# Graph attention, list building: adj added onto column fractions by the transfer itself, instead of a plain load, a conversion on ScalarE and a product on GpSimd

## The chip, the cores and the metric

The kernel runs on one core of one Trainium2 chip. The metric is the device time of one execution in microseconds (us). An execution can fall in a slower state; ratios and intervals use fast runs alone. The kernels before and after were compared first on one chip; the experiments ran later on two others, on which the kernel before takes 1408 to 1439 us, slow runs included, instead of 1363 to 1372. So an experiment's time is only compared with runs of the kernel before on the same chip, and stages are compared by the traces.

## The reference

```python
# x: 3327 x 1024 float32, adj: 3327 x 3327 int32, 0 or 1, symmetric, with ones on the diagonal, some 17 ones a row
h = jnp.maximum(_layernorm(x, axis=-1), 0.0)
f = h @ Wf + bf
g = h @ Wg + bg
e = jax.nn.relu(f @ g.T)
scores = jnp.where(adj > 0, e, NEG)
attention = jax.nn.softmax(scores, axis=1)
return x + attention @ (h @ W + bW)
```

## The kernel before

Because adj has few ones, the kernel does not form the 3327 x 3327 scores (a dense path for other inputs stands in the file and is not used here). **Stage 1** turns each 128-row tile of adj (26 tiles) into a list of up to 40 column numbers per row, normalises x into a table `hd` in DRAM, multiplies the two weight matrices, and ranks the rows by degree. **Stage 2** gathers the rows of `hd` by these lists, forms the dots, the softmax and the weighted sums, and projects. The change concerns stage 1. There, one tile of adj passes through four engines:

```python
kpool = pool1("key", 4)            # four buffers for r, 128 x 3327 float32
iotaj = c1.tile([P, N], FP, name="iotaj")       # 1, 2, ... 3327 in every row
held = p_c.tile([P, NBIN + KM], FP, name="held")  # p_c is PSUM
iotad, lst = held[:, :NBIN], held[:, NBIN:]

def degrees(t):
    n = rows(t)
    r = kpool.tile([P, N], FP, name="r")
    a = r.bitcast(I32)
    for b, m in pieces(t):
        nc.sync.dma_start(a[b : b + m], adj[t * P + b : t * P + b + m, :])
    # [cut: the last two tiles go in two parts]
    nc.scalar.activation(r[:n, b:e], a[:n, b:e], AF.Relu, accum_out=to)      # int32 to float32; the sum is the degree
    nc.gpsimd.tensor_mul(r[:n, b:e], r[:n, b:e], iotaj[:n, b:e])             # key: the column's number, or 0
    return r

def edges(t, r):
    n = rows(t)
    cand = cpool.tile([P, SEG * 8], FP, name="cand")
    for s in range(SEG):                        # 8 largest keys of each of 16 segments of 208 columns
        nc.vector.max(cand[:n, s * 8 : s * 8 + 8], r[:n, s * SW : min(N, (s + 1) * SW)])
    # [cut: count of keys above 0]
    for i in range(0, KM, 8):                   # the 40 largest of the 128 candidates, in order
        nc.vector.max(lst[:n, i : i + 8], cand[:n])
        if i + 8 < KM:
            nc.vector.match_replace(cand[:n], lst[:n, i : i + 8], cand[:n], 0.0)
    nc.vector.tensor_scalar(lst[:n], lst[:n], float(N), 1.0, op0=ALU.min, op1=ALU.max)
    nc.vector.tensor_scalar(pay[:n, t, :KM], lst[:n], -1.0, None, op0=ALU.add)
    # [cut: degree, and its one-hot row]

for t in range(NT):                             # NT = 26, LAG = 4
    r = degrees(t)
    normed(t)     # load of x, row statistics (odd tiles on DVE, even ones on ScalarE), store to hd
    edges(t, r)
    # [cut: ranks, stores of finished lists]
    if t < KD:                                  # KD = 8
        load_Wg(t)
    elif t < 2 * KD:
        make_A(t - KD)
    if t == 2 * KD:
        make_rows()   # bias rows: three tiny casts on DVE, some matmuls
# [cut: ranking of the rows; then stage 2, whose first act is a gather on GpSimd]
```

## Time and profile before

The time was 1364.33 us (median of 3 runs); the profiled run's span on the core was 1370.1 us. I call **seam** the moment at which GpSimd issues the first gather of stage 2: it ends stage 1. **DMA work** is the sum of the durations of all packets in the trace, divided by 16 engines.

| kernel before | us |
|---|---|
| last packet of adj ends | 237.2 |
| seam | 285.3 |
| length of stage 2 | 1084.8 |
| DMA work on adj | 117.3 |
| all DMA work until the last packet of adj | 207.5 |
| median packet of adj (13,308 bytes, one row) | 0.498 |

The stretches of the kernel before, which the prediction uses, read: start:end, length, then busy time of PE, weight loads, DVE, ACT and POOL with the number of instructions in brackets, the granted clock, the mean busy share of the DMA engines, and GB/s. The whole of stage 1 up to the last adj packet, in such a line:

```profile
15.00:237.00 222.00, 176.51 (x639) 109.60 (x639) 183.92 (x897) 155.03 (x234) 169.54 (x24) 0.97 0.87 329
```

DVE is busy for 184 of 222 us and the DMA engines for 0.87 of the time. How adj is loaded stands among the DMA issues (out<-in, issuing queue, operation, count, KB each, median us from issue to landing):

```profile
r<-in_adj_dram SPq DMA_DIRECT2D x25, 1663.5 KB, 9.0
```

### The profile page before, as it was taken

The page shows a single profiled execution, that of the slowest core. Times are in us where ns is not written, and L with a number is a line of the kernel's source. Part 1 is how long each engine was busy: PE and PEld are TensorE (multiplying, and loading weights), DVE is VectorE, ACT ScalarE, POOL GpSimd, SP SyncE. Part 2 cuts the span into 40 slices and gives each one's busy share as a digit, 9 for nine tenths or more (in the row PEclk, how much of TensorE's full clock was granted, in tenths as well). Part 3 has the DMA queues.
Part 4 walks back from the last instruction along what each step waited for, and adds up shares of the span by engine and source line. Part 5 has one row for each costly group of instructions (what it writes and reads, how often), then busy time and mean ns, then how long its engine had stood idle before and what let it go on. Part 6 is the DMA issues. An engine that isn't in the chain of part 4 may idle for free.

```text
span 1370.1 us, 14184 instructions
## 1 busy us (share of the span) xinstructions
PE 1154.2 (84%) x4355; PEld 676.0 (49%) x4355; DVE 1218.5 (89%) x2595; ACT 489.2 (36%) x774; POOL 875.0 (64%) x628
## 2 busy tenths in 40 slices
PE   4669899246467998999999999999979999999784
PEld 3545454124244564656555555555545555555331
DVE  4888888928869999999999899999999999999970
ACT  6677676501042542344433233333322222221110
POOL 7787778435456766677667767776656667666411
PEclk9999999568689999999999999999999999999897
DMA  9887898268558989898989988988877889888612
GB/s 367 356 336 281 320 351 276 68 257 327 172 166 302 348 294 320 299 334 292 309 290 311 303 269 312 302 294 296 272 240 250 255 281 306 272 271 285 198 32 63
DMA packets 97711, 372.52 MB, mean 272 GB/s; under 512 B 14269, under 2 KB 14685, under 8 KB 94298
## 3 DMA queue, kind: packets, MB, share of 16 engines
q0 software_dynamic: 79552, 286.85, 62.4%
q1 hardware_dynamic: 10860, 70.49, 13.6%
q10 hardware_dynamic: 7212, 14.18, 2.9%
q8 instruction: 36, 0.59, 0.2%
q14 instruction: 51, 0.41, 0.1%
HBM read 343.67 MB, written 27.80 MB: 271 GB/s over the span
## 4 chain that ended last, share of the span: by engine, by line
PE 43%; issue 14%; DVE 9%; DMA 4%; POOL 4%; ACT 2%; POOLq 0%; ACTq 0%; DVEq 0%
PE ps_q L666 18%; PE ps_o L758 17%; PE yT_ps L724 6%; DVE G L746 5%; DMA G<-hd,pi 4%; POOL G L637 3%; DVE junk L683 3%; PE ps_q L667 1%; PE ps_o L759 1%; ACT hT L650 1%; DMA pi<-pd,perm 1%; PE ps_t L649 1%; DVE sc L683 1%; POOL res L637 0%; ACT q L668 0%
## 5 line engine op out<-in xcount | busy, mean ns | idle before, releaser
L637 POOL DMA_INDIRECT G<-hd,pi x468 | 541.2, 1156 | 220.2 <-issue 93.5
L683 DVE CUSTOM_DVE_ANT_0 junk<-G,q 128x1024 bf16<-128x1024 f32 x468 | 599.4, 1281 | 35.3 <-ACT q L668 18.1
L666 PE MATMUL ps_q<-A_sb,hT 128*128 128x342 f32 x1248 | 399.2, 467 | 59.4 <-ACT q L668 41.8
L746 DVE SCALAR_TENSOR_TENSOR G<-G,sc 128x1024 f32<-128x1024 f32 x320 | 410.8, 1284 | 4.6 <-ACT G L744 4.1
L758 PE MATMUL ps_o<-W_sb,yT 128*128 128x512 f32 x832 | 374.8, 604 | 4.4 <-ACT yT L753 4.4
L666 PEld LDWEIGHTS ps_q<-A_sb,hT 128*128 128x128 f32 x1248 | 231.8, 194 | 177.6 <-ACT q L668 43.7
L758 PEld LDWEIGHTS ps_o<-W_sb,yT 128*128 128x128 f32 x832 | 156.5, 192 | 195.4 <-issue 182.3
L436 POOL TENSOR_TENSOR r<-r,iotaj 128x3327 f32<-128x3327 f32 (+4 forms) x28 | 188.6, 6743 | 66.6 <-ACT r L435 51.7
L724 PE MATMUL yT_ps<-ident,G 128*128 128x128 f32 x1184 | 146.2, 279 | 24.7 <-DVE sc L708 8.2
L446 DVE MAX8 cand<-r 128x8 f32<-128x208 f32 (+2 forms) x416 | 134.4, 361 | 35.2 <-POOL r L436 35.2
L724 PEld LDWEIGHTS yT_ps<-ident,G 128*128 128x128 f32 x1184 | 133.8, 143 | 41.8 <-issue 15.7
L760 ACT COPY res<-ps_o 128x512 f32<-128x512 f32 x52 | 30.4, 585 | 298.9 <-PE ps_o L759 298.9
L740 ACT ACTIVATE G<-G,sc 128x1024 f32<-128x1024 f32 x122 | 129.2, 1135 | 0.0
L668 ACT COPY q<-ps_q 128x342 f32<-128x342 f32 x78 | 33.5, 447 | 244.8 <-DVE sc L683 135.9
L519 PE MATMUL ps_A<-WgT,WfT 128*128 128x512 f32 x256 | 118.5, 623 | 2.7 <-ACT WfT L490 2.6
L637 POOL DMA_INDIRECT res<-in_x_dram,perm x26 | 46.2, 1776 | 67.4 <-ACT res L760 62.8
L519 PEld LDWEIGHTS ps_A<-WgT,WfT 128*128 128x128 f32 x256 | 50.6, 200 | 65.1 <-issue 61.2
L768 POOL DMA_INDIRECT out_dram<-res,perm x25 | 34.5, 1378 | 72.5 <-DMA res<-in_x_dram,perm 72.5
L435 ACT ACTIVATE r<-r 128x3327 f32<-128x3327 int32 (+4 forms) x28 | 77.5, 2768 | 0.1
L650 ACT COPY hT<-ps_t 128x512 f32<-128x512 f32 x52 | 28.9, 590 | 59.2 <-PE ps_t L649 32.0
L637 POOL DMA_INDIRECT hp<-hd,perm x26 | 26.8, 1032 | 35.0 <-DVE final L612 21.2
L649 PE MATMUL ps_t<-ident,hp 128*128 128x128 f32 x208 | 31.2, 292 | 15.7 <-issue 10.8
(137 smaller groups left out, 743.9 us busy)
## 6 DMA issues: line engine op xcount, KB each, us to landing
r<-in_adj_dram SPq DMA_DIRECT2D x25, 1663.5 KB, 9.0
xt<-in_x_dram SPq DMA_DIRECT2D x25, 512.0 KB, 9.8
hd<-xt ACTq DMA_DIRECT2D x25, 512.0 KB, 6.8
G<-hd,pi POOLq DMA_INDIRECT x468, 6.1
wr<-in_L_gnn_Wg_dram SPq DMA_DIRECT2D x8, 512.0 KB, 13.9
wr<-in_L_gnn_Wf_dram SPq DMA_DIRECT2D x8, 512.0 KB, 9.6
W_sb<-in_L_gnn_W_dram SPq DMA_DIRECT2D x1, 4096.0 KB, 16.3
r<-in_adj_dram SPq DMA_DIRECT2D x1, 1455.6 KB, 8.8
```

The lines of the kernel that those rows point to most:

```text
L435: nc.scalar.activation(r[:n, b:e], a[:n, b:e], AF.Relu, accum_out=to)
L436: nc.gpsimd.tensor_mul(r[:n, b:e], r[:n, b:e], iotaj[:n, b:e])
L446: nc.vector.max(cand[:n, s * 8 : s * 8 + 8], r[:n, s * SW : min(N, (s + 1) * SW)])
L519: nc.tensor.matmul(ps, WfT[:, k, :], WgT[:, k, o * CB : (o + 1) * CB], start=(k == 0), stop=(k == KD - 1))
L637: return nc.gpsimd.indirect_dma_start(out=to, out_offset=None, in_=table, in_offset=bass.IndirectOffsetOnAxis(ap=idx, axis=0), **kw,)
L649: nc.tensor.transpose(ps[:, k, :], of[:, (g + k) * P : (g + k + 1) * P], ident)
L666: nc.tensor.matmul(ps[:, :QB], hT[:, k, :], A_sb[:, k, o : o + QB], start=(k == 0), stop=False)
L683: nc.vector.tensor_tensor_reduce(junk, g, e["q"][:, :D], 1.0, e["q"][:, D : D + 1], op0=ALU.mult, op1=ALU.add, accum_out=e["sc"][:, k : k ...
L724: nc.tensor.matmul(e["yT"][:, c, :], g[:, c * P : (c + 1) * P], ident, is_transpose=True, start=(first and c % 4 == 0), stop=(last and c % ...
L740: nc.scalar.activation(g, g, AF.Copy, scale=p)
L746: nc.vector.scalar_tensor_tensor(y, g, p, y, op0=ALU.mult, op1=ALU.add)
L758: nc.tensor.matmul(ps, yT[:, k, :], W_sb[:, k, o * CB : (o + 1) * CB], start=(k == 0), stop=False)
```

## The change

The intent is to take work off the engines: the column fractions j/4096 are copied into the buffer, and the load of adj, cast from int32 to float32 on its way, is **added** onto them. What lands is the key: 1 + j/4096 for an edge, j/4096 otherwise. ScalarE then only counts signs of (key - 1), into another tile and beside DVE; GpSimd's product, and ScalarE's place between load and DVE, are gone.

```diff
+KEY = 4096.0
+        nc.vector.tensor_scalar(iotaj, iotaj, 1.0 / KEY, None, op0=ALU.mult)
-        def degrees(t):
+        def keys(t):
             n = rows(t)
             r = kpool.tile([P, N], FP, name="r")
-            a = r.bitcast(I32)
+            nc.gpsimd.tensor_copy(r[:n], iotaj[:n])
             for b, m in pieces(t):
-                nc.sync.dma_start(a[b : b + m], adj[t * P + b : t * P + b + m, :])
-            [cut: the last two tiles in two parts]
-                nc.scalar.activation(r[:n, b:e], a[:n, b:e], AF.Relu, accum_out=to)
-                nc.gpsimd.tensor_mul(r[:n, b:e], r[:n, b:e], iotaj[:n, b:e])
+                for c, e in ((0, SEG // 2 * SW), (SEG // 2 * SW, N)):
+                    nc.gpsimd.dma_start(
+                        r[b : b + m, c:e], adj[t * P + b : t * P + b + m, c:e], accum_op=ALU.add
+                    )
+            sign = lnj.tile([P, N], BF, name="sign")
+            nc.scalar.activation(sign[:n], r[:n], AF.Sign, bias=minus1[:n], accum_out=deg[:n, t : t + 1])
             return r
 [cut: the buffers minus1 and tops]
 [cut: count of keys above 1.0 instead of 0.0]
-            nc.vector.tensor_scalar(lst[:n], lst[:n], float(N), 1.0, op0=ALU.min, op1=ALU.max)
-            nc.vector.tensor_scalar(pay[:n, t, :KM], lst[:n], -1.0, None, op0=ALU.add)
+            nc.scalar.copy(tops[:n, t : t + 1], lst[:n, 0:1])
+            ids = cpool.tile([P, KM], FP, name="ids")
+            nc.vector.tensor_scalar(ids[:n], lst[:n], 1.0 + N / KEY, 1.0 + 1 / KEY, op0=ALU.min, op1=ALU.max)
+            nc.vector.tensor_scalar(pay[:n, t, :KM], ids[:n], KEY, -KEY - 1.0, op0=ALU.mult, op1=ALU.add)
 [cut: the degree is kept as 2 x degree - N, its uses are adapted]
-            r = degrees(t)
+            r = keys(t)
```

More of the change, by code (lines that the diff above doesn't have):

```diff
@@ L367, in edge_path @@
         nc.gpsimd.iota(iotaj, pattern=[[1, N]], base=1, channel_multiplier=0, allow_small_or_imprecise_dtypes=True)
+        nc.vector.tensor_scalar(iotaj, iotaj, 1.0 / KEY, None, op0=ALU.mult)
+        minus1 = c1.tile([P, 1], FP, name="minus1")
+        nc.gpsimd.memset(minus1, -1.0)
         iotap = c1.tile([P, P], FP, name="iotap")
@@ L372, in edge_path @@
         iotad, lst = held[:, :NBIN], held[:, NBIN:]
-        nc.vector.tensor_copy(iotad, iotap[:, :NBIN])
+        nc.vector.tensor_scalar(iotad, iotap[:, :NBIN], 2.0, -float(N), op0=ALU.mult, op1=ALU.add)
         part = c1.tile([P, 1], FP, name="part_no")
@@ L383, in edge_path @@
         deg = c1.tile([P, NT], FP, name="deg")
-        half = c1.tile([P, 1], FP, name="half")
+        tops = c1.tile([P, NT], FP, name="tops")
         cnt = c1.tile([P, NT], FP, name="cnt")
@@ L387, in edge_path @@
         oh = c1.tile([P, NT, NBIN], BF, name="oh")
-        nc.gpsimd.memset(deg, 1.0)
+        nc.gpsimd.memset(deg, 2.0 - N)
+        nc.gpsimd.memset(tops, 0.0)
         nc.gpsimd.memset(cnt, 1.0)
@@ L423, in normed @@
                 nc.scalar.dma_start(hd[t * P + a : t * P + a + m, :], xt[a : a + m])
-        def degrees(t):
+        def keys(t):
             n = rows(t)
             r = kpool.tile([P, N], FP, name="r")
-            a = r.bitcast(I32)
+            nc.gpsimd.tensor_copy(r[:n], iotaj[:n])
             for b, m in pieces(t):
-                nc.sync.dma_start(a[b : b + m], adj[t * P + b : t * P + b + m, :])
-            cuts = [0, SEG // 2 * SW, N] if t >= NT - 2 else [0, N]
-            for i, (b, e) in enumerate(zip(cuts, cuts[1:])):
-                to = deg[:n, t : t + 1] if not i else half[:n]
-                nc.scalar.activation(r[:n, b:e], a[:n, b:e], AF.Relu, accum_out=to)
-                nc.gpsimd.tensor_mul(r[:n, b:e], r[:n, b:e], iotaj[:n, b:e])
-                if i:
-                    nc.scalar.activation(deg[:n, t : t + 1], deg[:n, t : t + 1], AF.Identity, bias=half[:n])
+                for c, e in ((0, SEG // 2 * SW), (SEG // 2 * SW, N)):
[4 more added lines that the diff above has]
+            nc.scalar.activation(sign[:n], r[:n], AF.Sign, bias=minus1[:n], accum_out=deg[:n, t : t + 1])
             return r
@@ L448, in edges @@
             nc.vector.tensor_scalar(
-                pos[:n], cand[:n], 0.0, None, op0=ALU.is_gt, op1=ALU.add, accum_out=cnt[:n, t : t + 1]
+                pos[:n], cand[:n], 1.0, None, op0=ALU.is_gt, op1=ALU.add, accum_out=cnt[:n, t : t + 1]
             )
@@ L454, in edges @@
                     nc.vector.match_replace(cand[:n], lst[:n, i : i + 8], cand[:n], 0.0)
-            nc.vector.tensor_scalar(lst[:n], lst[:n], float(N), 1.0, op0=ALU.min, op1=ALU.max)
-            nc.vector.tensor_scalar(pay[:n, t, :KM], lst[:n], -1.0, None, op0=ALU.add)
+            nc.scalar.copy(tops[:n, t : t + 1], lst[:n, 0:1])
+            ids = cpool.tile([P, KM], FP, name="ids")
+            nc.vector.tensor_scalar(ids[:n], lst[:n], 1.0 + N / KEY, 1.0 + 1 / KEY, op0=ALU.min, op1=ALU.max)
+            nc.vector.tensor_scalar(pay[:n, t, :KM], ids[:n], KEY, -KEY - 1.0, op0=ALU.mult, op1=ALU.add)
             dg = cpool.tile([P, 1], FP, name="dg")
-            nc.vector.tensor_scalar(dg[:n], deg[:n, t : t + 1], float(NBIN - 1), None, op0=ALU.min)
+            nc.vector.tensor_scalar(dg[:n], deg[:n, t : t + 1], 2.0 * (NBIN - 1) - N, None, op0=ALU.min)
             nc.vector.tensor_copy(pay[:n, t, KM : KM + 1], dg[:n])
@@ L613, in edge_path @@
         ne = c1.tile([P, NT], FP, name="ne")
+        nc.vector.tensor_scalar(cnt, cnt, 2.0, -float(N), op0=ALU.mult, op1=ALU.add)
         nc.vector.tensor_tensor(ne, deg, cnt, op=ALU.not_equal)
+        nc.vector.tensor_scalar(tops, tops, 2.0, None, op0=ALU.is_ge)
+        nc.vector.tensor_max(ne, ne, tops)
         nc.vector.tensor_reduce(bads[:, NT : NT + 1], ne, AX.X, ALU.max)
-        nc.vector.tensor_scalar(ne, deg, 1.0, None, op0=ALU.is_lt)
+        nc.vector.tensor_scalar(ne, deg, 2.0 - N, None, op0=ALU.is_lt)
         nc.vector.tensor_reduce(bads[:, NT + 1 : NT + 2], ne, AX.X, ALU.max)
@@ L669, in prepare @@
         df = small.tile([P, 1], FP, name="df")
-        nc.vector.tensor_copy(df, pi[:, KM : KM + 1])
+        nc.vector.tensor_scalar(df, pi[:, KM : KM + 1], 0.5, N / 2, op0=ALU.mult, op1=ALU.add)
         nc.vector.tensor_scalar(bads[: rows(s), s : s + 1], df[: rows(s)], float(CAPS[s]), None, op0=ALU.is_gt)
```

## The prediction

> **What bounds the kernel now.** I first read the page's busy slices, then the busy time of the engines by stretches, then the waits of the first stage. The program has two stages. In the first, 26 tiles of adj (128 x 3327) become lists of keys while x is normalised and the weights are multiplied; in the second, rows are gathered by those lists. The change touches the first stage only (and one instruction per tile in the second). The seam is visible in the waits: GpSimd sits idle until `final`, then issues the first gather of the second stage, 285.3 us into the span (timeline of GpSimd).
>
> Stretches of the kernel before (start:end, length, then busy us of PE, weight loads, DVE, ACT, POOL; granted clock, DMA share, GB/s):
>
> ```profile
> 15.00:35.00 20.00, 11.69 (x55) 11.08 (x54) 13.34 (x56) 16.08 (x25) 18.10 (x3) 1.00 1.02 419
> 35.00:75.00 40.00, 22.06 (x105) 20.52 (x104) 33.19 (x169) 26.70 (x41) 28.73 (x5) 1.00 0.86 333
> ...
> 195.00:240.00 45.00, 42.33 (x138) 21.70 (x137) 39.29 (x195) 30.11 (x49) 35.48 (x5) 0.96 0.85 282
> 240.00:266.00 26.00, 6.44 (x61) 4.96 (x60) 25.05 (x110) 17.60 (x34) 14.76 (x4) 0.62 0.16 61
> 266.00:286.00 20.00, 2.76 (x35) 1.76 (x34) 16.24 (x52) 0.00 (x0) 0.67 (x1) 0.50 0.16 35
> ```
>
> The reader is to see that until 240 us both DVE (83 to 87%) and the DMA engines (0.85 to 1.02) are nearly full, and that from 240 to 286 us only DVE works: the last lists and the ranking. DVE's only large wait, and the loads' largest, are these:
>
> ```profile
> DVE cand L446 <- POOL r L436: 35.2, 15, 3.7
> ```
>
> ```profile
> SPq L430 <- DVE cand L446: 64.1, 9, 11.3
> ```
>
> So DVE waits 35.2 us in all for GpSimd's product, and the adj loads wait for DVE to free one of four buffers. The product itself, from the page:
>
> ```profile
> L436 POOL TENSOR_TENSOR r<-r,iotaj 128x3327 f32<-128x3327 f32 (+4 forms) x28 | 188.6, 6743 | 66.6 <-ACT r L435 51.7
> L446 DVE MAX8 cand<-r 128x8 f32<-128x208 f32 (+2 forms) x416 | 134.4, 361 | 35.2 <-POOL r L436 35.2
> ```
>
> The obvious prize is those 35 us. What counts against it is how little room the DMA engines have. Queues of the first 260 us (packets, MB, share of 16 engines):
>
> ```profile
> q1 hardware_dynamic: 9820, 66.30, 67.4%
> q10 hardware_dynamic: 6096, 13.00, 13.7%
> ```
>
> That is 0.674 x 260 = 175 us for adj, x and the weights, and 36 us for writing hd: 211 us of a stage whose loads end near 240.
>
> **What the Trainium skill says.** "DMA: Bandwidth & Descriptors", section SWDGE vs HWDGE vs iDMA: accumulating and casting transfers can only be issued from GpSimd; that is why the load moves there. The kernel before has accumulating gathers issued by GpSimd (res += x), but none that casts. The same page, SDMA does more than copy: the adding unit reduces two streams and takes at most 2048 elements on trn2, which fits the split of a row into 1664 + 1663; it gives no rate, so the trace decides (next part). The same page, Issuing engines are not separate DMA queues: all issuers share the same 16 engines, so moving the load off SyncE gains no bandwidth; the trace agrees, the share never passing 1.08. "SBUF — State Buffer", Who interferes with whom: some DVE copies and GpSimd instructions lock each other out of a shared port. The trace agrees: a DVE cast of 17 columns took 3.53 us at 247.3 us, beside a 3.68 us product.
>
> **The change part by part.**
> 1. GpSimd's product goes (188.6 us in all, 7.2 us a tile). In its place comes a copy of the fractions into r. It has one input; the nearest duration is the iota of the same shape, 2.91 us, so I estimate 3 us a tile, 78 us in all. Added are two DMA issues a tile: an accumulating gather cost GpSimd 1.58 us (median of 26), so about 3 us a tile. GpSimd then spends about 6 us a tile and is no bound.
> 2. ScalarE's Relu (2.96 us) becomes Sign over as many elements: the same, plus a 0.2 us copy. But it no longer stands between load and DVE: the old chain was load, Relu 3.0, product 7.2, DVE; the new is copy 3, load, DVE.
> 3. DVE keeps its counts of MAX8 and match-replace, so its 8.3 us a tile stays (173.5 us busy in 35 to 240 us, in which 21 tiles pass). One 3327-wide scaling and a few tiny operations at the end add some 4 us, mostly where DVE waits anyway.
> 4. The adj load becomes an add: each byte is read from HBM, the destination is read too, and the sum is written. The price is to be had from the accumulating gathers of the second stage. Stretches of plain gathers (296), of moments when the accumulating ones fill the engines (443, 536, 861), and of the last one, alone (1355):
>
> ```profile
> 296.00:310.00 14.00, 14.00 (x43) 8.39 (x42) 0.21 (x2) 2.03 (x4) 10.64 (x12) 0.83 1.02 409
> 443.00:444.00 1.00, 0.00 (x0) 0.00 (x0) 1.00 (x2) 0.00 (x0) 0.38 (x1) 1.00 1.07 213
> 536.00:537.00 1.00, 1.00 (x3) 0.65 (x4) 1.00 (x3) 0.19 (x1) 0.26 (x1) 0.63 1.08 209
> 861.00:862.00 1.00, 0.35 (x1) 0.30 (x2) 1.00 (x4) 1.00 (x3) 0.00 (x0) 1.00 1.05 217
> 1355.00:1357.00 2.00, 0.00 (x0) 0.00 (x0) 0.00 (x0) 0.00 (x0) 0.00 (x0) 0.61 0.99 197
> ```
>
> Full engines move 409 GB/s of plain rows and about 200 GB/s (per unit of share) of added rows; in the packet records a 4096-byte packet takes 159 ns plain and 328 ns added. It is occupancy, not latency: with other gathers queued the share stays at 1.07, and the bytes halve. adj has 3327 x 3327 x 4 = 44.3 MB, so 44.3 / 0.200 = 221 us of all 16 engines. It was 44.3 / 66.3 x 175 = 117 us. **This adds about 104 us of DMA time to a stage that had 211 of 240 filled.**
>
> The sum: other traffic stays, 211 - 117 = 94 us; with 221 that is 315 us. The first add needs iota, scaling and copy and won't start before about 20 us; until then x and weights can fill perhaps 12 us, so 8 us are lost. With the engines 98% filled (they are now the bound; saturated stretches show 1.02) the last adj lands at 315 / 0.98 + 8 = 329 us. What follows it is DVE's: its first MAX8 of the last tile began at 260.5 us and the first gather went out at 285.3, so 25 us; at 354 us instead of 285 the second stage starts, 69 us later. For a fill above 1.00, as in the saturated stretches, it would be 62 or less. I take +64. The second stage stays as it is. 1364.3 + 64 = 1428 us.
>
> **Rivals.** (a) The intent comes true: adding costs what plain loads cost. Then DVE bounds, 26 x 8.3 = 216 us, plus some 25 before its first tile and 14 of ranking: 255 instead of 285, 1335 us. For it: DVE's 35 us of waits. Against: every accumulating gather of the trace. (b) DMA engines overlap the two reads better in long rows (6656 bytes against 4096) and fill to 1.06: 300 us at most of work, 25 to 30 us over the old stage, 1390 us, within 2%. (c) The cast, which nothing in this trace prices, slows the unit further: at half the rate again, 221 us more, above 1600 us. (d) A handshake: in the new program's order GpSimd copies two tiles, then issues their four adds; both copies wait for DVE. A pair would take copy 3 + issue 1.5 + two loads of 8.5 to 12 us + DVE 8.3 after the second, at most 37 us over two pair slots, 18.4 a pair; the DMA bound is 315 / 13 = 24 us a pair, so it hides, at worst 20 us more: 1450.
>
> **Range and chances.** From a fill of 1.06 (+47) less some luck, to a fill of 0.90 with handshake (+100): 1393 to 1465 us. Slower by over 2% (above 1391.6): 0.87, since even the full-speed case lies there. Within 2%: 0.08, for (b). Faster: 0.05, for (a).
>
> **What would show it.** Right: r<-adj packets near 530 ns for 6656 bytes (328 x 6656 / 4096) in the software queue, DMA share near 1.0 but only 250 to 290 GB/s to about 325 us, DVE waiting for adj transfers instead of GpSimd, first gather of the second stage near 350 us, and a second stage as long as before (1085 us). Wrong: packets near 250 ns (rival a), or well over 600 ns (rival c), or a DMA share below 0.85 with GpSimd's copies or issues named in the waits (rival d), or a second stage that changes its length.

## The result, and the profile after

The changed kernel is correct and slower: 1416.68 us (median of 4 runs, 1415.39 to 1418.06) against 1366.74 (median of 4, 1363.25 to 1369.9). The ratio is 1.0366, with a 95% interval of 1.0333 to 1.0399. Ratios here are the mean time of one kernel's fast runs over the mean of the other's of the same rounds, so not quite the ratio of the medians. The profiled runs' spans on the core were 1416.1 and 1370.1 us.

| | before | after | predicted for after |
|---|---|---|---|
| DMA work on adj, us | 117.3 | 215.9 | 221 |
| all DMA work until the last packet of adj, us | 207.5 | 313.7 | 315 |
| last packet of adj ends, us | 237.2 | 306.8 | 329 |
| from there to the seam, us | 48.1 | 25.3 | 25 |
| seam, us | 285.3 | 332.1 | 354 |
| length of stage 2, us | 1084.8 | 1083.9 | as before |

Stretches of the kernel after, with the same columns; the first two lines make up the time until the last adj packet:

```profile
0.00:15.00 15.00, 5.37 (x26) 4.77 (x26) 4.91 (x11) 10.64 (x19) 11.51 (x32) 1.00 0.88 288
15.00:307.00 292.00, 185.11 (x695) 112.23 (x695) 206.94 (x995) 171.53 (x275) 119.70 (x79) 0.74 1.03 257
307.00:332.00 25.00, 2.87 (x35) 1.77 (x34) 22.29 (x80) 5.01 (x6) 0.00 (x0) 0.50 0.17 56
...
332.10:1416.00 1083.90, 963.04 (x3604) 555.41 (x3604) 986.73 (x1515) 308.67 (x495) 681.55 (x572) 0.95 0.80 269
```

The DMA engines went from 0.87 busy at 329 GB/s to **1.03 busy at only 257 GB/s**: full, and slower per byte. DVE, 83% busy before (184 of 222 us), is now at 71% (207 of 292). TensorE's granted clock fell as well, from 0.97 to 0.74, but TensorE is busy for only 185 of the 292 us, and DVE waits for it 1.6 us in all of stage 1. The pages' slices show the same, first before (34.3 us each, the first eight in stage 1), then after (35.4 us each, the first nine):

```profile
DVE  4888888928869999999999899999999999999970
...
DMA  9887898268558989898989988988877889888612
```

```profile
DVE  3658865893887999999999989999998999999980
...
DMA  9999999986856898889999878888867888888712
GB/s 292 268 266 253 260 260 249 227 204 238 328 182 195 303 348 307 277 308 319 308 326 314 305 246 289 298 290 297 287 218 270 272 280 283 277 273 287 230 31 61
```

DMA stands at 9 for eight slices, and DVE, which stood at 8 or 9 in seven of eight before, falls to 5 or 6 in four of nine. The groups that replaced the product show that the engines' part of the intent did come true:

```profile
L436 POOL COPY r<-iotaj 128x3327 f32<-128x3327 f32 (+1 forms) x26 | 78.2, 3064 | 157.6 <-DVE dg L465 68.3
...
L443 ACT ACTIVATE sign<-r,minus 128x3327 bf16<-128x3327 f32 (+1 forms) x26 | 79.8, 3069 | 43.8 <-DMA r<-in_adj_dram 41.9
```

GpSimd spends 78.2 us on copies where it spent 188.6 on products, and sits idle for 157.6 us before them. DVE no longer waits for it; its waits of stage 1 are now mostly for transfers (and 11.0 us for ScalarE's small copy of `tops`):

```profile
DVE st L413 <- DMA xt<-in_x_dram: 66.4, 11, 11.6
...
DVE cand L451 <- DMA r<-in_adj_dram: 16.7, 10, 3.8
```

The larger wait is for x, not for adj. Those x transfers are issued late because their five buffers come free only when the stores to `hd` have landed. The queue of the loads waited for these stores 20.2 us in the kernel before and 216.2 us after, and a store's median time from issue to landing rose from 6.8 to 10.6 us (first before, then after):

```profile
SPq L400 <- DMA hd<-xt: 20.2, 7, 7.3
hd<-xt ACTq DMA_DIRECT2D x25, 512.0 KB, 6.8
```

```profile
SPq L407 <- DMA hd<-xt: 216.2, 21, 24.5
hd<-xt ACTq DMA_DIRECT2D x25, 512.0 KB, 10.6
```

An add now takes this long from its issue to its landing:

```profile
r<-in_adj_dram POOLq DMA_DIRECT2D x25, 832.0 KB, 21.1
r<-in_adj_dram POOLq DMA_DIRECT2D x25, 831.5 KB, 26.3
```

Half a tile takes 21.1 to 26.3 us, where a whole one took 9.0. Most of that is queueing: a packet, one half row of 6656 bytes, has a median of 515 ns, so 128 of them over 16 engines would take 4.1 us alone (an estimate).

### The profile page after: what moved, and what is told of

The parts are those of the page before. It is cut to its first block, busy times and chain, and to the rows that moved or that the text cites. A ratio compares the mean times of both kernels' runs of the same rounds, so it can differ in the third digit from the quotient of the medians.

```text
span 1416.1 us, 14277 instructions
## 1 busy us (share of the span) xinstructions
PE 1156.4 (82%) x4355; PEld 674.2 (48%) x4355; DVE 1220.9 (86%) x2599; ACT 495.8 (35%) x794; POOL 812.8 (57%) x682
## 4 chain that ended last, share of the span: by engine, by line
PE 38%; DMA 19%; DVE 18%; issue 15%; POOL 5%; ACT 3%; POOLq 0%; SPq 0%; ACTq 0%; DVEq 0%
PE ps_q L677 16%; PE ps_o L769 15%; DVE G L757 6%; DMA xt<-in_x_dram 6%; DMA hd<-xt 5%; PE yT_ps L735 5%; DMA G<-hd,pi 4%; POOL G L648 4%; DVE cand L451 3%; DVE junk L694 3%; DMA r<-in_adj_dram 2%; DVE cand L459 1%; DVE held L457 1%; ACT G L751 1%; DMA pi<-pd,perm 1%
## 5 line engine op out<-in xcount | busy, mean ns | idle before, releaser
L436 POOL COPY r<-iotaj 128x3327 f32<-128x3327 f32 (+1 forms) x26 | 78.2, 3064 | 157.6 <-DVE dg L465 68.3
L451 DVE MAX8 cand<-r 128x8 f32<-128x208 f32 (+2 forms) x416 | 131.9, 360 | 16.7 <-DMA r<-in_adj_dram 16.7
L526 PE MATMUL ps_A<-WgT,WfT 128*128 128x512 f32 x256 | 124.9, 650 | 5.6 <-ACT WfT L497 5.6
L443 ACT ACTIVATE sign<-r,minus 128x3327 bf16<-128x3327 f32 (+1 forms) x26 | 79.8, 3069 | 43.8 <-DMA r<-in_adj_dram 41.9
L779 POOL DMA_INDIRECT out_dram<-res,perm x25 | 38.9, 1556 | 70.9 <-DMA res<-in_x_dram,perm 70.9
L413 DVE BATCH_NORM_STATS2 st<-xt 128x6 f32<-128x512 f32 (+1 forms) x26 | 17.6, 685 | 66.4 <-DMA xt<-in_x_dram 66.4
L479 PE MATMUL pre<-oh,low 128*128 128x64 bf16 x26 | 5.4, 209 | 68.7 <-DVE hit L476 68.7
## 6 DMA issues: line engine op xcount, KB each, us to landing
r<-in_adj_dram POOLq DMA_DIRECT2D x25, 832.0 KB, 21.1
r<-in_adj_dram POOLq DMA_DIRECT2D x25, 831.5 KB, 26.3
hd<-xt ACTq DMA_DIRECT2D x25, 512.0 KB, 10.6
```

Source lines behind the costliest of these rows:

```text
L436: nc.gpsimd.tensor_copy(r[:n], iotaj[:n])
L443: nc.scalar.activation(sign[:n], r[:n], AF.Sign, bias=minus1[:n], accum_out=deg[:n, t : t + 1])
L526: nc.tensor.matmul(ps, WfT[:, k, :], WgT[:, k, o * CB : (o + 1) * CB], start=(k == 0), stop=(k == KD - 1))
L779: ins = nc.gpsimd.indirect_dma_start(out=out[:, :], out_offset=bass.IndirectOffsetOnAxis(ap=perm[:, s : s + 1] if s < N // P else final, a ...
```

## The experiments

My theory was that the accumulating transfer costs twice the engines' time per byte, that the DMA engines are therefore the bound of stage 1, and that all else hides behind them. Against it stood: that the cast, not the addition, is what costs; that moving the issue to GpSimd costs (a handshake between its copies or products and the loads); that `ids` in SBUF makes DVE wait for GpSimd; and that DVE's new waits for x are the loss. All twelve runs gave correct results; code that is left out of a diff is marked `[cut]`. e1 to e11 ran on one chip, e12 on another.

### e1: the cast alone

The kernel before, its load issued by GpSimd in the same two halves and cast on its way; ScalarE's pass and the product are kept.

```diff
-            a = r.bitcast(I32)
+            a = r
             for b, m in pieces(t):
-                nc.sync.dma_start(a[b : b + m], adj[t * P + b : t * P + b + m, :])
+                for c, e in ((0, SEG // 2 * SW), (SEG // 2 * SW, N)):
+                    nc.gpsimd.dma_start(a[b : b + m, c:e], adj[t * P + b : t * P + b + m, c:e])
```

> The kernel before, with adj loaded by GpSimd in two casting halves (int32 to float32), nothing added. Theory (the read of the destination is the whole price): packets of 6656 bytes take about 250 ns (half of the 498 ns that a plain 13308-byte row took), 108 us of 16 engines in all. Rival 1 (the cast is the price) and rival 2 (the software queue or the halves are the price): packets near 515 ns, as in the changed kernel. The time is no evidence here: GpSimd's loads now queue behind its products, so it may well be slower than before (1380 to 1500).

Queue of the adj transfers in the first 299 us (packets, MB, share of 16 engines):

```profile
q0 software_dynamic: 7616, 44.29, 44.8%
```

The median packet took 268 ns. A plain row of 13,308 bytes took 498, so half a row would be 249 (an estimate): the cast from GpSimd costs 8% in halves. Still, the seam came at 329.9 us, and the one timed run took 1492.07 (median before 1419.54, two slow runs among its seven), with the engines only 0.776 busy. **With nothing added, the seam moved nearly as far as by the whole change.** The waits say how: GpSimd issues a load only after the products that stand ahead of it, so GpSimd waited 77.8 us for ScalarE, and ScalarE 77.0 for adj. That is a handshake, not a full engine. e1 itself does not part this order from the issuer, the cast and the halves; e12, which casts whole rows from GpSimd two tiles ahead and has its seam at 279.9 us, shows that issuer and cast need not cost this. It makes the share of the engines the thing to look at in all that follows.

### e2: the addition alone

The kernel before, its buffer set to zero and adj added as int32, without a cast.

```diff
             a = r.bitcast(I32)
+            nc.gpsimd.memset(r[:n], 0.0)
             for b, m in pieces(t):
-                nc.sync.dma_start(a[b : b + m], adj[t * P + b : t * P + b + m, :])
+                for c, e in ((0, SEG // 2 * SW), (SEG // 2 * SW, N)):
+                    nc.gpsimd.dma_start(
+                        a[b : b + m, c:e], adj[t * P + b : t * P + b + m, c:e], accum_op=ALU.add
+                    )
```

> The kernel before, with r cleared by GpSimd and adj added into it as int32, no cast. Theory: packets of 6656 bytes take about 515 ns, 216 us of 16 engines, as in the changed kernel. Rival 1 (the cast is the price): near 250 ns. Rival 2 (software queue): 515 here too, but then also in e1. The time is no evidence: clearing, two issues and product together load GpSimd with over 12 us a tile (1420 to 1520).

The same queue, in the first 479 us:

```profile
q0 software_dynamic: 7616, 44.29, 47.8%
```

That is the same 7616 packets and 44.29 MB in 0.478 x 479 = 229 us of all engines, where e1 needed 0.448 x 299 = 134. The median packet took 516 ns, against 268 cast only and 515 in the kernel after. In e2 the engines are not full (0.695), so the 516 ns are not a queue's doing. **It is the addition that nearly doubles a packet's time; the cast on top of it adds nothing that these numbers show.** By all engines' time the factor is smaller, 229 against 134 and, in the kernels after and before, 215.9 against 117.3 us, or 1.84: the packets that add nothing have a longer tail (mean 564 ns beside the median of 498 in the kernel before). GpSimd pays too: its issue of half a tile takes a median of 0.57 us in e1, 1.19 in e2 and 1.49 with cast and addition in the kernel after. The time, 1656.3 us with the seam at 508.3, says nothing about the change: the memset, the adds, ScalarE's pass and the product followed one another.

### e3 and e7: the addition on half of each row

To see whether less DMA work gives time back, e3 adds only the first 1664 columns. The rest is loaded with a cast, two tiles ahead, and multiplied by 1 + j/4096 on GpSimd, which gives the same keys for the edges.

```diff
[cut: 1 is added to the second half of iotaj; the loop calls load(t + 2) before keys(t)]
+        def load(t):
[cut]
+            nc.gpsimd.tensor_copy(r[:n, :h], iotaj[:n, :h])
+            for b, m in pieces(t):
+                nc.gpsimd.dma_start(r[b : b + m, h:], adj[t * P + b : t * P + b + m, h:])
+                nc.gpsimd.dma_start(r[b : b + m, :h], adj[t * P + b : t * P + b + m, :h], accum_op=ALU.add)
         def keys(t):
[cut: the copy and the adds of the kernel after]
+            nc.gpsimd.tensor_mul(r[:n, h:], r[:n, h:], iotaj[:n, h:])
```

> The changed kernel, but only the first 1664 columns of adj are added; the rest are loaded by a casting transfer that adds nothing, two tiles ahead, and multiplied by 1 + fraction on GpSimd (half a product, 3.7 us a tile). Theory (DMA occupancy sets the stage's end): 314 - 50 = 264 us of DMA work at a share of 1.04 is 254 us plus 25 of tail; the first gather of the second stage near 280 to 288, the time within 1% of the kernel before (1355 to 1375). Rival 3 (the handshake of GpSimd's paired copies and issues, not the occupancy, lengthens the stage): GpSimd has as much to do as before the halving, so the time stays near 1400 to 1417.

The expectation failed. DMA work fell as it should, to 185.0 us on adj and 282.1 in all, but the seam came later than in the kernel after, at 355.7 us, and the time was 1.0491 of that before (1.037 to 1.0611). With the share at 0.905 another bound had taken over. One part of it stood in the groups: the DVE cast of the finished lists took a mean of 1158 ns. So e7 repeats it with `ids` in PSUM:

```diff
-        held = p_c.tile([P, NBIN + KM], FP, name="held")
-        iotad, lst = held[:, :NBIN], held[:, NBIN:]
+        held = p_c.tile([P, NBIN + 2 * KM], FP, name="held")
+        iotad, lst, ids = held[:, :NBIN], held[:, NBIN : NBIN + KM], held[:, NBIN + KM :]
...
-            ids = cpool.tile([P, KM], FP, name="ids")
```

> e3, with ids in PSUM. Theory (occupancy of the DMA engines): DMA work is 264 us, at a share near 1.0 the first gather goes out at 280 to 292 us, between e6 and the changed kernel. Rival (handshake in GpSimd's queue, which now mixes copy, two issues and a product): DMA share stays near 0.9 and the seam above 310, as in e3.

The seam moved to 327.1 us and the time to 1.0235 (1.0114 to 1.0357): better than e3, 5 us of seam better than the kernel after, and still far from the expected 280 to 292. DMA work was 32 us below that of the kernel after, and 5 us of it came back. The expectation's rival, a seam above 310, came true in its number. DVE now waited 68.2 us for x, and GpSimd 61.4 us for ScalarE's sums of signs, which points to the order of instructions; no run tests that for e7.

### e4 and e6: no addition at all

Whole rows, loaded with a cast two tiles ahead and multiplied by 1 + j/4096 on GpSimd. The sum of signs stays beside DVE.

```diff
[cut: 1 is added to iotaj; the loop calls load(t + 2) before keys(t)]
+        def load(t):
[cut]
+            for b, m in pieces(t):
+                nc.gpsimd.dma_start(r[b : b + m], adj[t * P + b : t * P + b + m, :])
         def keys(t):
-            nc.gpsimd.tensor_copy(r[:n], iotaj[:n])
-            for b, m in pieces(t):
-                for c, e in ((0, SEG // 2 * SW), (SEG // 2 * SW, N)):
-                    nc.gpsimd.dma_start([cut], accum_op=ALU.add)
+            nc.gpsimd.tensor_mul(r[:n], r[:n], iotaj[:n])
```

> The changed kernel without the add: a casting transfer loads whole rows two tiles ahead, GpSimd multiplies by 1 + fraction (7.2 us a tile), ScalarE's sum of signs beside DVE. Theory: DMA work is back at some 208 us, ScalarE is out of the chain, and DVE (8.3 us a tile), GpSimd (8.2) and DMA (8.0) are all near one another; first gather of the second stage near 260 to 280, time 1340 to 1360, up to 2% below the kernel before. Rival 3 or any theory in which the changed kernel's loss lies in its GpSimd order or in ScalarE's Sign and not in the add: stays above 1390.

Missed again: the seam came at 337.9 us, the time was 1.0436 (1.0342 to 1.053), although DMA work fell to 224.9 us and the last adj packet landed at 273.8. Much of the cause is in one small group (e6 will show 30 us). Groups of DVE, first in e4 and then in the kernel after (line, engine, operation, out<-in, count, then busy us and mean ns of one):

```profile
L467 DVE TENSOR_SCALAR pay<-ids 128x40 int32<-128x40 f32 x25 | 68.5, 2741 | 0.0
```

```profile
L463 DVE TENSOR_SCALAR pay<-ids 128x40 int32<-128x40 f32 x25 | 9.8, 391 | 0.0
```

In the kernel before, the same cast from PSUM takes 180 ns. From SBUF, beside a GpSimd that multiplies for 188 of the first 288 us, it takes a mean of 2741 and up to 23,700 ns. The longest, from 263.8 to 287.5 us, ends with the last of three products in a row. It is the lock of which the prediction spoke (the Trainium skill, "SBUF — State Buffer", Who interferes with whom). To test that, e6 moves `ids` to PSUM, with the edit of e7:

> e4, with the 40 clamped keys (ids) kept in PSUM instead of SBUF. In e4 the conversion of ids to the payload took 2741 ns a tile (180 ns in the kernel before, from PSUM) and DVE was 100% busy. Theory: DVE's SBUF-to-SBUF operation waits for GpSimd's product on a port that they share; from PSUM it takes 180 ns again, DVE needs 8.3 us a tile, and the first gather goes out at 258 to 272 us, some 65 to 80 us earlier than in e4, and 1 to 2% below the kernel before. Rival: the conversion is slow for another reason, or GpSimd's product is what sets the pace; then ids stay slow or the seam stays above 300.

The same cast in e6, where `ids` is a part of `held` (ns: least, median, most; then first and last start in us):

```profile
L466 DVE TENSOR_SCALAR pay<-held x26: 173/181/200, 59.7 to 293.3; 128x40 int32<-128x40 f32 x25, 127x40 int32<-127x40 f32 x1
```

The seam came at 308.0 us, and the time was 1.0221 (1.0066 to 1.0377). What the lock had cost in e4 was 30 us of seam. The expected 258 to 272 was missed, and the rival's "above 300" met. The trace puts 43.2 us of DVE's waits down to x; e10 tests whether they are the reason.

### e5: the kernel before again

A profile of the unchanged kernel on the experiments' chip.

> The kernel before, unchanged, profiled on the chip of this call: on the chip of the last call its runs took 1408 to 1439 us instead of 1364, so stages must be compared on one chip. If the first stage is as long as in the first profile (first gather of the second stage at 285 us, within 6) and only the second is longer, the slower chip loses its time in the gathers, and e3 and e4 did lengthen the first stage (e4's first gather went out at 337.9 us, against an expected 260 to 280). If the first stage is longer too (over 300), e3 and e4 can't be judged from their times.

The seam came at 285.2 us and the last adj packet at 236.9, as on the first chip (285.3 and 237.2); only stage 2 was longer, 1129.0 us against 1084.8. So the seams of e1 to e11 can be compared with each other and with those of the first chip; that this holds on e12's chip too is assumed, as no kernel before was profiled there.

### e8: the kernel after with ids in PSUM

Was the lock part of the loss? Only the edit of e7, made to the kernel after.

> The changed kernel with ids in PSUM and nothing else. Its conversion took 391 ns instead of 180, so about 5 us of DVE come back. Theory: the DMA engines set the end of the stage (share 1.04 throughout), so the seam stays within 5 us of 332 and the time within 0.5% of the changed kernel (ratio to the kernel before 1.030 to 1.038). Rival (the port lock is part of the loss): 10 us or more gained.

The cast fell from 391 to 183 ns, and the seam stayed: 331.3 us against 332.1. DMA work was 313.8 us, and the share 1.021. The measured ratio was 1.0274 (1.015 to 1.0399), an interval that holds the first one's 1.0366, but itself just under the expected 1.030 to 1.038. The ratios of e6, e7 and e8 lean on four runs of the kernel before (1420.5 to 1436.3 us) of which three, pooled later with those of other rounds, count as slow; against the mean of the seven that count as fast (1417.2) all three would be 1.032 to 1.033. The seam is the better witness. **The lock that cost e4 30 us of seam costs the changed kernel 0.8 us in these profiles**, and the waits for x took up what was gained: 83.4 us instead of 66.4.

### e9: the kernel after without waits for x in DVE's order

Were DVE's 66.4 us of waits for x the loss? Here the row statistics of odd tiles go to ScalarE too, so that no DVE instruction waits for x directly.

```diff
-            if t % 2:
+            if t < 0:
```

> The changed kernel with the row statistics of the odd tiles on ScalarE, as those of the even tiles are, so that DVE no longer stands in line for x. In the changed kernel DVE's largest wait is not for adj (16.7 us) but for x (66.4 us). Theory (the adds fill the DMA engines and set the end, the waits for x are only where DVE happens to stand): DMA work stays at 314 us, share 1.02 to 1.04, and the first gather stays within 6 us of 332. Rival 4 (the order of instructions, DVE queued behind late x loads, is what lengthens the stage): it falls by 20 us or more, towards 300.

Waits and one stretch of e9:

```profile
DVE cand L451 <- DMA r<-in_adj_dram: 57.1, 25, 6.8
```

```profile
195.00:240.00 45.00, 39.50 (x149) 21.77 (x148) 31.29 (x148) 31.78 (x54) 18.61 (x12) 0.92 1.04 260
```

The waits for x went, and waits for adj took their place: 57.1 us where there had been 16.7. The engines stayed full at 1.04 and 260 GB/s, and the seam came at 334.8 us. DVE had been freed of work and nothing was won, which is what a bound elsewhere looks like. The edit is not free, though: ScalarE does more, and in e11 it costs the kernel before 23 us of seam. So the last packet of adj is the cleaner sign here: 303.0 us against 306.8, at 310.8 us of DMA work against 313.7. The tail after it grew from 25.3 to 31.8 us. Which transfer a wait is put down to depends on the order of the instructions that wait.

### e10, e11 and e12: is there something to be had without the addition?

e6 still waited for x. e10 gives it the edit of e9, and e11 is the control: the same edit made to the kernel before.

> e6 (casting load, product on GpSimd, ids in PSUM) with the same edit. In e6 DMA had only 222 us of work to 265 us, and DVE stood 43 us waiting for x. Theory: here the order matters, as the DMA engines are not full: DVE's waits for x vanish, the first gather moves from 308 to 265 to 290 us, and the kernel is level with the one before or up to 1.5% faster. Rival: GpSimd's mixed queue of loads and products holds it back; then the seam stays above 300.

> The kernel before with the same edit alone, as the control for e9 and e10. Its DVE waits for x only 0.6 us, so little should move: DVE loses about 1.5 us of work a pair of tiles, ScalarE gains 2.4; first gather at 275 to 292, time within 1% of the kernel before.

e10's seam came at 302.8 us (ratio 1.0166, 1.0081 to 1.0252). It missed the expected 265 to 290 although DVE's waits for x were gone and adj had landed at 235.9: with the waits went only 5 us of seam. The timeline of DVE in e10 (start, length) shows one instruction of 17 columns that stood for 20 us:

```profile
228.22 20.43 DVE L551 CAST terms<-cols 128x17 bf16<-128x17 f32 x1
```

It is the same lock, once: a tiny cast of the bias rows that GpSimd's products, three in a row, kept out. e11 was worse than the kernel before, with the seam at 308.1 us (ratio 1.0153, 1.0062 to 1.0244); in its order ScalarE's added work seems to delay the Relu, on which the product waits (69.1 us), and on that DVE, 49.2 us instead of 35.7 in e5:

```profile
DVE cand L446 <- POOL r L436: 49.2, 23, 7.0
```

In these runs, then, the edit gained 5 us where ScalarE does not stand ahead of the product and lost 23 where it does. e12 is e10 with `make_rows()` moved behind the loop, where GpSimd has nothing left to multiply (its last product ends at 247.9 us, the casts start at 260.5):

```diff
-            if t == 2 * KD:
-                make_rows()
         for t in range(NT - LAG, NT):
             counted(t)
+        make_rows()
```

> e10 with the bias rows (make_rows) emitted after the tiles instead of in the middle. In e10 one DVE cast of 17 columns, from SBUF to SBUF, took 20.43 us (228.2 to 248.6 us) while GpSimd made three products in a row, and ScalarE stood 22.5 us behind it. Theory (port lock): no DVE operation beside the products is then over 4 us, the first gather goes out some 20 us earlier, at 275 to 288 us, and the kernel is level with the one before (within 1%), perhaps up to 1% faster. Rival (GpSimd's mixed queue of loads and products is too slow by itself): the seam stays above 295 us and the time 1% or more above the kernel before.

In e12 the three casts together took 0.5 us, and the seam came at 279.9 us, 5 us before that of the kernel before in e5. But the time, in five rounds, was 1.0085 of it (1.0031 to 1.0138): medians 1443.86 against 1431.95 us, two slow runs in the latter. In the profiled run stage 2 took 1165 us, against 1129 in e5 on another chip. Over all variants stage 2 took from 1121 us (e8) to 1165 us (e12) in the profiled runs, though at most one small instruction a tile differs there. The work is the same (DVE busy for 986.1 us of stage 2 in e5, 987.1 in e12), so on DVE it is waits that grew. Why, and whether by more than the chips' noise, is not settled. It can hide a gain: the fast runs of e6, e7 and e8 average 1462 to 1464 us, although their seams lie at 308.0, 327.1 and 331.3. **No version was shown to beat the kernel before.** What e12 does show, beside e9, is the price of the addition in stage 1: with the loads cast and multiplied instead of added, DMA work until the last adj packet goes from 310.8 to 220.1 us, that packet from 303.0 to 237.2, and the seam from 334.8 to 279.9. The same stretch of e12, to be read against that of e9:

```profile
195.00:240.00 45.00, 30.04 (x126) 16.27 (x125) 37.69 (x192) 37.76 (x59) 40.85 (x11) 0.82 0.87 267
```

DVE, ScalarE and GpSimd are busier than in e9, and the engines no longer full. e12 also loads whole rows instead of halves, two tiles ahead, and differs in the place of `ids` and of the bias rows. e8 showed `ids` to be worth 1 us in the kernel after; the bias rows were worth 23 us in e12 against e10, but their three casts took only 0.17 us each in e9.

| run | DMA work to last adj, us | share | last adj, us | seam, us | ratio |
|---|---|---|---|---|---|
| e5, before | 206.7 | 0.87 | 236.9 | 285.2 | one look |
| e1, cast only | 232.1 | 0.78 | 298.9 | 329.9 | one look |
| e2, addition only | 332.5 | 0.70 | 478.1 | 508.3 | one look |
| e3, half added | 282.1 | 0.91 | 311.6 | 355.7 | 1.0491 |
| e7, e3 with ids in PSUM | 281.5 | 0.97 | 291.4 | 327.1 | 1.0235 |
| e4, cast and product | 224.9 | 0.82 | 273.8 | 337.9 | 1.0436 |
| e6, e4 with ids in PSUM | 221.6 | 0.84 | 265.0 | 308.0 | 1.0221 |
| e8, after with ids in PSUM | 313.8 | 1.02 | 307.3 | 331.3 | 1.0274 |
| e9, after, statistics on ScalarE | 310.8 | 1.03 | 303.0 | 334.8 | 1.0383 |
| e10, e6, statistics on ScalarE | 216.3 | 0.92 | 235.9 | 302.8 | 1.0166 |
| e11, before, statistics on ScalarE | 212.5 | 0.82 | 260.1 | 308.1 | 1.0153 |
| e12, e10 with late bias rows | 220.1 | 0.93 | 237.2 | 279.9 | 1.0085 |

Only e8 and e9 have full DMA engines, as the kernel after has; there the seam equals the last packet plus 24 to 32 us. In the rows with a share of 0.97 or less, DMA work does not order the seams. There a lock accounts for what e7 gained over e3, e6 over e4 and e12 over e10; for the rest the waits point to the order of instructions, and no run tests it alone.

## Why the prediction was right, point by point

- **The price of the addition: right.** The gathers of stage 2 had given it (4096 bytes in 328 ns), scaled to 533 ns for 6656 bytes; 515 were measured. Adj took 215.9 us of all engines instead of 221. e2 shows that it is the addition, and e1 that it is not the cast.
- **The other traffic, and the sum: right.** 313.7 us of work against 315.
- **The fill: the step that was mis-sized.** "With the engines 98% filled ... the last adj lands at 315 / 0.98 + 8 = 329 us." Measured: 306.8, 22 us earlier. The 8 us lost at the start shrank to under 2: the first packet of adj did start at 20.7 us, but until 20 us the share was 0.92, which is 18.4 us of work and not 12, since x, the weights and the first stores to `hd` were there to move. From 20 to 307 us it was 1.03. Over the whole it is 313.7 / 306.8 = 1.02; 315 / 0.98 is 321 and 315 / 1.02 is 309, so by this split the fill makes up 12 to 13 us of the difference, the start 8, and the sum of the work 1. The saturated stretches of stage 2, which the prediction quotes with 1.05 to 1.08, had been the better guide. Rival (b) asked for a fill of 1.06, which was not reached, and its sum is off: 315 / 1.06 + 8 + 25 is 330 us, 45 over the old seam and not 25 to 30. The range's own +47 for that fill meets the measured +46 by luck: the fill was lower, and the lost start was not lost.
- **The tail: right.** 25.3 us from the last packet to the seam.
- **From seam to time: right in kind.** The seam moved by 46.8 us, stage 2 by -0.9, the span by 46.0 and the medians by 49.9. Predicted were +64; the 15 to 18 us too many are those of the fill and the start.
- **The gain on the engines: right that it is hidden.** GpSimd's copies took 78.2 us as estimated (78), its issues a median of 1.49 us. DVE's 35 us of waits for the product are gone and longer ones for transfers took their place. e8 and e9 took a lock and the waits for x away from DVE and moved the seam by -0.8 and +2.7 us.
- **"DVE waiting for adj transfers instead of GpSimd": right in kind, wrong in name.** It waited 66.4 us for x and 16.7 for adj. e9 shows that these can be exchanged for each other.
- **The rivals.** (a) fell with the 515 ns, (c) with e1 and e2. (d), the handshake, did not set the pace in the changed kernel, whose engines were full. e1, whose order is another one, shows that such a handshake can cost 45 us of seam where they are not.
- **Readings of the lines that were off.** "Until 240 us" DVE was busy for 67% in the first stretch quoted (13.34 of 20 us) and for 81 to 87% in the others, and the DMA share fell to 0.81 in one left out (115 to 155 us). From 240 to 266 us not only DVE worked: ScalarE was busy for 17.60 and GpSimd for 14.76 of 26 us. The share does pass 1.08 in single microseconds (1.80 from 199 to 200 us, as packets count where they start), though over the 15 us around it, 190 to 205, it is 1.00. None of these enters the sum.

What stays open: why stage 2 was longer in most experiments, in e12 above all, what of e1's 45 us is order, and how the seam depends on DMA work between e7 (281.5 us, seam 327.1) and the kernel after (313.7, seam 332.1), where two bounds lie close together.

## What to carry to other kernels

Before work is moved from an engine into a transfer, add up the transfers' time on the DMA engines in that stage and price the new form from one of its kind in the trace, by packet duration: an accumulating load took 1.84 times the engines' time for the same bytes (by median packet, twice), and this stage had room for 30 us, not for 100. When engines become the bound, estimate their fill from stretches of the same trace that are saturated, not from caution. When a version with less work on the bound is not faster, look for the next one in tiny instructions with absurd durations and in the order of issue before doubting the theory.

## What the Trainium skill lacked or had wrong

- "DMA: Bandwidth & Descriptors", SDMA does more than copy, gives no rate for the addition; the half rate in "Collectives: The Full Stack", Part 3: Why 7× under link rate, is for reductions of collectives, not for a load added onto a tile. The runs show 515 to 516 ns for 6656 bytes, against 268 with a cast alone: about half the rate, some 205 GB/s over 16 engines (44.28 MB in 215.9 us) against 378 (44.28 MB in 117.3 us) for the plain load of the kernel before.
- The same page, SWDGE vs HWDGE vs iDMA, says that casts must go through GpSimd but not what they cost. The runs show medians of 513 ns against 498 for a row of 13,308 bytes (e4 and the kernel before), 3%, and of 268 ns for 6656 bytes (e1), some 8% above half of the plain row. By all engines' time the casting rows took 127.2 us against 117.3, but plain rows took 124.4 in e11, so that most of this is not the cast's.
- "SBUF — State Buffer", Who interferes with whom, describes the lock between some DVE instructions and GpSimd as one that lasts for an instruction. The trace agrees that there is one, but the wait can outlast several: a 17-column cast stood for 20.43 us (e10) and a 40-column one for up to 23.7 us (e4), where one product takes 7.24 us. Where the input lay in PSUM the same operation kept its 180 ns.
- No page that I read says what the order of issue costs when GpSimd issues loads and computes too: in e1, where the load was also cast and halved, the seam moved from 285 to 330 us with the DMA engines only 0.78 busy.
